# A delta-rule attention and ternary FFN kernel: the ternary product moved ahead of F's turn, and half of the values' product into the place it leaves

## The chip, the cores and the metric

The kernel runs on one core of one Trainium2 chip. The metric is the device time of one launch, in microseconds (us). The engines are TensorE (PE; its weight loads are shown as PEld), VectorE (DVE), ScalarE (ACT), GpSimd (POOL) and SyncE (SP), which here issues the DMAs. All arithmetic is in 32-bit floats.

## The reference

The input x is 4 sequences of 4096 tokens of 512 channels. Two blocks follow each other, each with a layernorm before it, a layernorm of its output, and a residual sum.

```python
def attn(x):                      # 16 heads of 32 channels
    rk = heads(x) / norm(heads(x));  wk = rk one token later
    v = heads(x @ Wv.T);  gate = sigmoid(x @ Wg.T);  beta = sigmoid(x @ Wb.T)
    # over the tokens, per sequence and head, S is 32 x 32:
    err = (v_t - wk_t @ S) * beta_t;  S = S + outer(wk_t, err);  o_t = (rk_t @ S) * gate_t
    return o @ Wo.T
def ffn(x):
    xn = layernorm(x) * ln_gamma + ln_beta
    w_q = clip(round(weight / mean(abs(weight))), -1, 1)        # ternary
    return clip(xn * 128 / max(abs(xn)), ...) @ w_q * scale
x = x + layernorm(attn(layernorm(x)))
x = x + layernorm(ffn(layernorm(x)))
```

## The kernel before

The token loop is cut into 128 units of 32 tokens. A unit holds all 4 sequences, so that its tokens fill the 128 partitions (4 x 32), and its 512 channels are the free dimension. Within a unit the recurrence is solved as a block: a triangular 32 x 32 matrix per sequence and head is inverted, and then only the state S (`state`) goes from unit to unit.

Two streams of units run side by side. The "unit of the blocks" (`AHEAD`, number k) does what doesn't need the state: the layernorm and the keys (`keys`, `keys_turn`: product `ps_hT`), the values and gates (`values`: `ps_v` at L251, 288 columns with both gates; `values_rest`: `ps_v` at L279, 256 columns; `values_out` multiplies each half by the key norms on DVE, L267), the Gram matrices of the keys (`grams`, L319), their copy out of PSUM on ACT (`blocks`, L330), and their masking on POOL (`writes` makes the mask `mb`, L290 to L294, from the gate tile `gb` of ACT, L256; `masked` applies it, L338). The "chain's unit" (`BACK`, number i, some 20 units behind) does what needs the state: `predict` (product `ps_r`, L439, and the difference `r` on DVE, L445), `apply` (the inverse times r: `ps_u`, L455, copied out as `ft` by ACT), `errors` (F's turn: the transposition `ps_f`, L468, from which DVE makes `e`, L471, and `o`, L476), `outputs` (o times the gate, POOL, L480), and `grow` (product `ps_ds`, L491, and four additions to the state on DVE, L497). Units behind the chain's unit are carried on through the output product (`project`, `ps_wo`, L534), the first residual (`residual`, DVE, L543, which needs `rstd_b` of POOL), the second norm, the ternary product (`ternary_a` and `ternary_b`, two of the four `ps_y` matmuls each, L593) and the second residual (`finish`, DVE, L612, with `rstd_y` of POOL).

The inverses of several units (8 in the steady stretch) are made together on DVE, as 30 pairs of a product `pr` (L364) and a sum `na` (L370), and one copy of a diagonal (L375). They are spread over 8 steps: `inverses(share)` in the plan issues the next instructions until the share of the step is used up. An instruction isn't cut, so a share runs over by up to one instruction, and the next one begins later for it.

The order is written out by hand. For each step the tuple `plan` is walked, and each function's instructions are chained behind those before it on the same engine, so each engine runs its own instructions in the plan's order and waits by semaphores for the other engines. The first steps that have a chain's unit are double: each is followed by the tuple `beside`, which does one more unit of the blocks. From some 20 units before the end the tuple `late` is used, which has no unit of the blocks.

PSUM is held as four single banks (tag `bank`) and one group of four banks (tag `quad`, for `ps_gram` and `ps_ds` in turn). A product waits until the last reader of the bank it is given has finished.

Of the kernel before, what the change touches and what calls it, by code (L numbers as in the profile page):

```python
# [22 lines left out]
def kernel(  # L23
# [91 lines left out]
    with ExitStack() as ph1:  # L115
# [35 lines left out]
        half = D // 2  # L151
# [535 lines left out]
        def ternary_centre():  # L687
# [13 lines left out]
        BACK, AHEAD = "chain's unit", "unit of the blocks"  # L701
# [3 lines left out]
            (BACK, -3, x1_turn),  # L705
            (BACK, 0, apply), (BACK, -3, x1_scale), (AHEAD, -1, masked),
            (AHEAD, 1, key_sums), (AHEAD, 3, x_stats), (AHEAD, 1, key_norms),
            (AHEAD, 2, keys), (AHEAD, 2, key_squares), 0.38,
            (BACK, -4, ternary_a), (BACK, 0, errors), (BACK, -4, ternary_b), (BACK, 0, outputs),
            (AHEAD, 3, x_norm), 0.2, (BACK, 0, grow), (BACK, -2, x1_stats),  # L710
            (AHEAD, 2, keys_turn), (AHEAD, -1, gates_first), (AHEAD, -2, gates), (BACK, 1, rekey), (BACK, -4, finish),
            (BACK, -1, project), (BACK, -3, largest), 0.36, (BACK, -2, x1_norm),
            (BACK, -1, residual), (AHEAD, 0, values), (AHEAD, 0, values_out, half),
            (AHEAD, 0, writes), (AHEAD, 0, values_rest), 0.06, (AHEAD, 0, values_out, 0),
            (AHEAD, 0, grams),
        )

        late = (
# [282 lines left out]
```

## Time and profile before

| | us |
|---|---|
| median of 3 runs | 2315.33 (2312.81 to 2315.37) |
| the profiled execution | 2311.62 |
| its span, first to last instruction | 2309.9 |
| PE busy | 2219.5 (96%) |
| DVE busy | 2027.3 (88%) |
| ACT busy | 1554.6 (67%) |
| POOL busy | 1528.3 (66%) |
| 16 DMA engines, mean share in q1 | 71.7% |

The mean granted clock of TensorE is 0.986. A busy time is a sum over stages with different limits. The page's slices show a start of some 130 us before the chain's first unit, a stretch of double steps up to about 320 us, single steps with a few stalls up to about 510 us, a steady stretch up to about 1976 us, and the late steps and the end.

### The profile page before, as it was taken

What the parts mean: (1) busy time and instruction counts of PE and PEld (TensorE: products, weight loads), DVE (VectorE), ACT (ScalarE), POOL (GpSimd) and SP (SyncE); (2) the same over time, 40 slices, a digit from 0 to 9 for tenths busy, and PEclk for the clock granted to TensorE, in tenths of its full rate; (3) what the DMA queues carried; (4) which work ended last, traced back from release to release, by engine and by line L of the source; (5) the groups of instructions that cost most, each with busy time, mean ns of one, the idle gap of its engine ahead of it and who ended that gap; (6) DMA issues with size and microseconds to landing.
All of it is one profiled execution on the core that took longest, in us unless ns stands there. A gap on an engine that the chain in (4) does not pass through costs nothing.

```text
span 2309.9 us, 60163 instructions
## 1 busy us (share of the span) xinstructions
PE 2219.5 (96%) x22563; PEld 1450.3 (63%) x22563; DVE 2027.3 (88%) x3069; ACT 1554.6 (67%) x3613; POOL 1528.3 (66%) x2057
## 2 busy tenths in 40 slices
PE   6688999999999999999999999999999999999997
PEld 5565666666666666666666666666666666655553
DVE  6898988999898998989989898899899898899853
ACT  6556676776776767767767677676776767655554
POOL 5787886777776776767767677676776766532221
PEclk9889999999999999999999999999999999999999
DMA  5586686777868777787877778677886967666652
GB/s 171 134 215 190 190 215 205 190 196 206 198 198 205 206 193 211 194 201 216 188 210 201 201 197 204 212 189 208 203 207 196 207 206 191 182 174 179 179 162 81
DMA packets 757202, 445.29 MB, mean 193 GB/s; under 512 B 582928, under 2 KB 582928, under 8 KB 756912
## 3 DMA queue, kind: packets, MB, share of 16 engines
q1 hardware_dynamic: 756528, 440.92, 71.7%
q8 instruction: 179, 2.93, 0.6%
q14 instruction: 111, 0.91, 0.1%
q10 hardware_dynamic: 384, 0.52, 0.1%
HBM read 205.07 MB, written 235.14 MB: 191 GB/s over the span
## 4 chain that ended last, share of the span: by engine, by line
PE 82%; DVE 11%; POOL 2%; issue 2%; DMA 2%; ACT 1%; SPq 1%; ACTq 0%; DVEq 0%; POOLq 0%
PE ps_wo L534 18%; PE ps_y L593 16%; PE ps_v L251 10%; PE ps_v L279 8%; PE ps_ds L491 6%; PE ps_gram L319 5%; PE ps_r L439 5%; PE ps_u L455 4%; DVE pr L364 3%; PE ps_hT L196 3%; PE ps_oT L514 2%; DVE na L370 2%; PE ps_f L468 2%; PE ps_xn L514 2%; DVE st_a L110 1%
## 5 line engine op out<-in xcount | busy, mean ns | idle before, releaser
L593 PE MATMUL ps_y<-wq,xn 128*128 128x512 f32 x1024 | 494.6, 606 | 0.0
L330 ACT COPY nat<-ps_gram 32x512 f32<-32x512 f32 x512 | 295.3, 577 | 286.6 <-PE ps_gram L319 276.1
L364 DVE TENSOR_TENSOR pr<-na 128x336 f32<-128x336 f32 (+25 forms) x540 | 461.2, 854 | 11.3
L370 DVE TENSOR_TENSOR na<-na,pr 128x336 f32<-128x336 f32 (+25 forms) x540 | 459.2, 850 | 12.2
L534 PE MATMUL ps_wo<-woT,oT 128*128 128x512 f32 x1024 | 464.0, 596 | 0.7 <-ACT oT L527 0.7
L231 POOL TENSOR_TENSOR rn<-ss,mhalf 128x16 f32<-128x16 f32 x128 | 440.7, 3443 | 10.7
L497 DVE TENSOR_TENSOR state<-ps_ds,state 32x512 f32<-32x512 f32 x508 | 348.4, 686 | 19.7 <-PE ps_ds L491 13.5
L338 POOL TENSOR_TENSOR nat<-nat,mb 128x512 f32<-128x512 f32 x122 | 159.5, 1307 | 290.6 <-issue 223.7
L534 PEld LDWEIGHTS ps_wo<-woT,oT 128*128 128x128 f32 x1024 | 185.3, 191 | 188.2 <-issue 184.7
L251 PE MATMUL ps_v<-wvbT,hN 128*128 128x288 f32 x1024 | 279.2, 417 | 14.3 <-POOL hN L207 14.2
L593 PEld LDWEIGHTS ps_y<-wq,xn 128*128 128x128 f32 x1024 | 174.5, 190 | 149.3 <-issue 146.0
L251 PEld LDWEIGHTS ps_v<-wvbT,hN 128*128 128x128 f32 x1024 | 198.1, 195 | 110.8 <-issue 28.2
L279 PE MATMUL ps_v<-wvbT,hN 128*128 128x256 f32 x1024 | 243.4, 381 | 0.0
L99 POOL TENSOR_TENSOR rstd_b<-vpe_b,mhalf 128x1 f32<-128x1 f32 x128 | 104.9, 820 | 186.3 <-ACT vpe_b L105 186.3
L279 PEld LDWEIGHTS ps_v<-wvbT,hN 128*128 128x128 f32 x1024 | 195.8, 191 | 34.3 <-DVE xr L543 0.4
L445 DVE TENSOR_TENSOR r<-v,ps_r 128x512 f32<-128x512 f32 x128 | 87.8, 686 | 135.0 <-PE ps_r L439 134.9
L520 ACT ACTIVATE junk_b<-ps_wo 128x512 f32<-128x512 f32 x128 | 76.5, 598 | 191.9 <-PE ps_wo L534 191.9
L491 PEld LDWEIGHTS ps_ds<-e,h 32*128 32x128 f32 x4064 | 127.3, 189 | 115.3 <-DVE e L471 91.1
L575 ACT ACTIVATE xn<-ps_xn,lnb,lng 128x128 f32<-128x128 f32 x512 | 193.6, 466 | 0.0
L491 PE MATMUL ps_ds<-e,h 32*128 32x128 f32 x4064 | 151.8, 286 | 19.3 <-DVE e L471 19.2
L319 PEld LDWEIGHTS ps_gram<-hT 32*128 32x128 f32 x4096 | 126.6, 187 | 39.5 <-issue 16.0
L319 PE MATMUL ps_gram<-hT 32*128 32x128 f32 x4096 | 151.1, 284 | 0.0
(153 smaller groups left out, 3867.6 us busy)
## 6 DMA issues: line engine op xcount, KB each, us to landing
x<-in_L_attn_x_dram SPq DMA_DIRECT2D x256, 128.0 KB
hT_d<-hT SPq DMA_DIRECT2D x128, 256.0 KB
v_d<-v SPq DMA_DIRECT2D x128, 256.0 KB
nat_d<-nat SPq DMA_DIRECT2D x128, 256.0 KB
na<-nat_d SPq DMA_DIRECT2D x256, 128.0 KB
q_d<-na SPq DMA_DIRECT2D x64, 512.0 KB
v<-v_d SPq DMA_DIRECT2D x128, 256.0 KB
hT<-hT_d SPq DMA_DIRECT2D x128, 256.0 KB
```

Of the source, the lines that this page charges most:

```text
L231: nc.gpsimd.tensor_tensor(rn, ss, mhalf, ALU.pow)
L251: nc.tensor.matmul(ps[:, : half + 2 * H], lhsT=my["hN"][:, k, :], rhs=wvbT[:, k, half:], start=(k == 0), stop=(k == KC - 1),)
L279: nc.tensor.matmul(ps[:, :half], lhsT=my["hN"][:, k, :], rhs=wvbT[:, k, :half], start=(k == 0), stop=(k == KC - 1),)
L319: nc.tensor.matmul(ps[:, j, q * P : (q + 1) * P], lhsT=hT[rows, q, :], rhs=hT[rows, q, :], start=True, stop=True,)
L330: nc.scalar.copy(nat[s].rearrange("p (j q) t -> p j q t", j=HQ), ps[s].rearrange("p j (q t) -> p j q t", q=NQ)[:, :, :, s],)
L364: nc.vector.tensor_tensor(prs[s], bcast(na[:, :, s, s + 1 :], [P, np_, s, m], 2), bcast(na[:, :, :s, s], [P, np_, s, m], 3), ALU.mult,)
L370: nc.vector.tensor_tensor(na[:, :, :s, s + 1 :], na[:, :, :s, s + 1 :], prs.pop(s), ALU.add)
L491: nc.tensor.matmul(psd[:, b, q * P : (q + 1) * P], lhsT=h[s, q * P : (q + 1) * P], rhs=e[s, q * P : (q + 1) * P], start=True, stop=True,)
L497: nc.vector.tensor_tensor(S[s, :, :, s], psd[s].rearrange("p b (q d) -> p b q d", q=NQ)[:, :, :, s], S[s, :, :, s], ALU.add,)
L534: nc.tensor.matmul(ps, lhsT=oT[:, k, :], rhs=woT[:, k, :], start=(k == 0), stop=(k == KC - 1))
L575: nc.scalar.activation(xn[:, k * P : (k + 1) * P], ps[:, k * P : (k + 1) * P], AF.Identity, bias=lnb[:, k : k + 1], scale=lng[:, k : k + 1],)
L593: nc.tensor.matmul(my["ps_y"], lhsT=my["xn"][:, k * P : (k + 1) * P], rhs=wq[:, k, :], start=(k == 0), stop=(k == KC - 1),)
```

## The change

Only the tuple `plan` is changed; the functions and the tuples `lead`, `beside` and `late` are as they were. The ternary product's four matmuls are issued together ahead of F's turn. `values`, which is the first half of the values' product with the gates, is issued behind F's turn. Its DVE part `values_out(half)` follows, ahead of the state's growth. `values_rest` is issued ahead of `residual`. The inverses' shares of a step go from 0.38, 0.2, 0.36, 0.06 to 0.48, 0.12, 0.34, 0.06.

```diff
-            (AHEAD, 2, keys), (AHEAD, 2, key_squares), 0.38,
-            (BACK, -4, ternary_a), (BACK, 0, errors), (BACK, -4, ternary_b), (BACK, 0, outputs),
-            (AHEAD, 3, x_norm), 0.2, (BACK, 0, grow), (BACK, -2, x1_stats),
-            (AHEAD, 2, keys_turn), (AHEAD, -1, gates_first), (AHEAD, -2, gates), (BACK, 1, rekey), (BACK, -4, finish),
-            (BACK, -1, project), (BACK, -3, largest), 0.36, (BACK, -2, x1_norm),
-            (BACK, -1, residual), (AHEAD, 0, values), (AHEAD, 0, values_out, half),
-            (AHEAD, 0, writes), (AHEAD, 0, values_rest), 0.06, (AHEAD, 0, values_out, 0),
-            (AHEAD, 0, grams),
+            (AHEAD, 2, keys), (AHEAD, 2, key_squares), 0.48,
+            (BACK, -4, ternary_a), (BACK, -4, ternary_b), (BACK, 0, errors), (AHEAD, 0, values),
+            (BACK, 0, outputs), (AHEAD, 3, x_norm), 0.12, (AHEAD, 0, values_out, half),
+            (BACK, 0, grow), (BACK, -2, x1_stats), (AHEAD, 2, keys_turn),
+            (AHEAD, -1, gates_first), (AHEAD, -2, gates), (BACK, 1, rekey), (BACK, -4, finish),
+            (BACK, -1, project), (BACK, -3, largest), 0.34, (BACK, -2, x1_norm),
+            (AHEAD, 0, values_rest), (BACK, -1, residual), (AHEAD, 0, writes), 0.06,
+            (AHEAD, 0, values_out, 0), (AHEAD, 0, grams),
```

## The prediction

> **What bounds the kernel now.** First the page: which engine is full.
>
> ```profile
> PE 2219.5 (96%) x22563; PEld 1450.3 (63%) x22563; DVE 2027.3 (88%) x3069; ACT 1554.6 (67%) x3613; POOL 1528.3 (66%) x2057
> ```
>
> TensorE is, with DVE next. Then busy time by stretches, to see where TensorE still idles (stretch, length, PE, PEld, DVE, ACT, POOL, clock, DMA share, GB/s).
>
> ```profile
> 130.00:320.00 190.00, 170.27 (x1776) 122.47 (x1776) 172.32 (x284) 125.15 (x277) 157.26 (x200) 0.95 0.76 198
> ...
> 510.50:1976.00 1465.50, 1463.44 (x15123) 958.21 (x15127) 1325.80 (x1937) 1033.57 (x2408) 1039.98 (x1376) 1.00 0.76 202
> ```
>
> In the 86 steady steps TensorE idles 2 us of 1465, so no order of the same products can gain there. From one `r` to the next a step takes 17.01 us, in one step of eight 17.25. The double steps (130 to 320) have 20 us of idle. Third, who waits for whom.
>
> ```profile
> DVE r L445 <- PE ps_r L439: 134.9, 113, 1.7
> ...
> PEld ps_ds L491 <- DVE e L471: 91.1, 95, 4.8
> ...
> PE ps_ds L491 <- DVE e L471: 19.2, 23, 4.6
> ```
>
> DVE waits for `ps_r` ahead of `r`, in 113 of 128 steps, 1.2 us each. This is DVE's whole reserve. If DVE is later than that, `ps_u`, which needs `r`, stops TensorE. Last, the timeline of DVE in the steady step with the least reserve, and of POOL at its end.
>
> ```profile
> 1090.06 0.69 DVE L445 TENSOR_TENSOR r<-v,ps_r 128x512 f32<-128x512 f32 x1 [1.38 <-PE ps_r L439]
> ...
> 1094.90 0.68 DVE L471 TENSOR_TENSOR e<-ps_f,bet 128x512 f32<-128x512 f32 x1
> ...
> 1097.27 2.79 DVE L497 TENSOR_TENSOR state<-ps_ds,state 32x512 f32<-32x512 f32 x4
> 1100.09 0.75 DVE L612 SCALAR_TENSOR_TENSOR xr<-ps_y,rstd_y,xr 128x512 f32<-128x512 f32 x1
> ...
> 1101.35 1.15 DVE L364 TENSOR_TENSOR pr<-na 128x960 f32<-128x960 f32 x1
> 1102.54 1.16 DVE L370 TENSOR_TENSOR na<-na,pr 128x960 f32<-128x960 f32 x1
> 1103.61 0.74 DVE L543 SCALAR_TENSOR_TENSOR xr<-ps_wo,rstd_b,xr 128x512 f32<-128x512 f32 x1
> 1104.27 0.41 DVE L267 TENSOR_TENSOR v<-ps_v,nrm 128x256 f32<-128x256 f32 x1
> 1104.61 1.64 DVE L364 TENSOR_TENSOR pr<-na 128x960 f32<-128x960 f32 x1
> 1106.17 0.41 DVE L267 TENSOR_TENSOR v<-ps_v,nrm 128x256 f32<-128x256 f32 x1
> 1107.08 0.69 DVE L445 TENSOR_TENSOR r<-v,ps_r 128x512 f32<-128x512 f32 x1 [0.50 <-PE ps_r L439]
> ```
>
> ```profile
> 1102.36 0.55 POOL L99 TENSOR_TENSOR rstd_b<-vpe_b,mhalf 128x1 f32<-128x1 f32 x1 [0.92 <-ACT vpe_b L105]
> 1103.48 0.30 POOL L290 TENSOR_TENSOR bet<-gb,rn 128x16 f32<-128x16 f32 x1 [0.57 <-ACT gb L256]
> ...
> 1104.15 1.08 POOL L294 TENSOR_TENSOR mb<-bet,mneg 128x512 f32<-128x512 f32 x1
> ...
> 1111.03 3.78 POOL L231 TENSOR_TENSOR rn<-ss,mhalf 128x16 f32<-128x16 f32 x1
> ```
>
> DVE is busy without a break from `r` to the wait of 0.50. The product at 1104.61 took 1.64 us where its like took 1.15: POOL's mask product ran from 1104.15 to 1105.23, and the inverse's product ended 1.02 after it.
>
> **The change, part by part, steady step.** Times count from the end of `r`; TensorE's slots are the start-to-start distances of the trace.
>
> *TensorE.* `ps_u` starts at 0.2, the ternary product at 1.2. Before: two matmuls 1.82, F's turn 0.44, two matmuls 1.81, so `ps_ds` at 5.3. After: four matmuls 3.53, F's turn at 4.7 for 0.44, half of the values (eight passes of 0.24, and 0.1) 2.0, so `ps_ds` at 7.2. Then `ps_ds` 1.10, `ps_hT` 0.50, `ps_wo` 3.44, other half 1.82, `ps_gram` 1.11, `ps_r` 1.01, `ps_oT` 0.49, `ps_xn` 0.53: 17.02 as before. Nothing is removed; nothing is gained but waits.
>
> *The wait for `e`.* DVE's 0.48 is about 0.7 us more of the inverse ahead of `e`. Summing each of the eight steps' instructions, DVE is ready for `e` at 4.2 to 5.35, F's turn ends at 5.3. So `e` starts near 5.37 and ends at 6.05, 1.2 us before `ps_ds`. The stall of 0.24 in one step of eight goes: 11 times 0.24, and two of 0.12, is -2.9.
>
> *The state's growth.* Its additions began 6.5 after `r`; now they can't begin before `ps_ds` has been made, 7.2 + 1.25 = 8.46 (1.25 is start of `ps_ds` to first addition where the addition waits). This is 1.94 later in the least-reserve step. `o` ends at 6.65, at most two pieces of the inverse and the 0.41 of the moved values' half fit before 8.46 (latest end 8.2), so these are free, but DVE idles up to 0.7 there.
>
> *From the growth to `r`.* DVE must be ready at 16.33, when `ps_r` is done. The growth to the end of the inverse's third share is unchanged in the step shown: additions 8.46, `finish` 11.28, maximum 11.94, product 12.54, sum 13.72 to 14.88, residual 14.79. Now the values' half is gone behind it (-0.33 by starts), so the piece of the last share starts at 15.46. POOL: `rstd_b` follows `ps_wo`, which ends 1.94 later, so it starts at 13.55 and ends at 14.1. `bet` no longer waits for `gb`, which is ready by 7.5. It is issued at once, but meets the sum of 13.72 to 14.88. In the trace such a small product of POOL ends 0.08 after DVE's instruction, and the mask follows 0.47 after that instruction (13.62 to 14.09 in the step from 1073.7): here at 15.35, 0.11 ahead of the piece at 15.46. So the mask goes first, until 16.43, and the piece ends 1.02 later, at 17.45; the last values' half 0.33 more: `r` at 17.7, 1.36 late. `ps_oT` and `ps_xn` cover 0.13. Stall 1.23 us, once in eight steps.
>
> In the step with the diagonal's copy, the copy of 0.41 meets the mask likewise: `r` at 16.6, stall 0.16. In the step with 0.98, 0.98 and 1.03 in the third share, 16.51: stall 0.05. The other five are ready at 15.5 to 16.0: none. Sum 1.44 x 11 = +15.8, with the -2.9: **+13**.
>
> *Steps from 320 to 510.* Here DVE is already last in three (17.9 to 19.2 us) and next to it in others. Where a piece stands behind the residual it meets the mask as above (0.5 to 1 each in five or six steps), and in others the later growth adds 0.6. I sum +6; bounds 0 and +9.
>
> *Double steps.* There `ps_ds` waits up to 2.9 us for `e`, and the values' half, moved into that wait, no longer stands between it and the next `ps_r`. At most 1.94 comes out of each. But DVE, or POOL at `rstd_y` and `rstd_b`, is next: by the step from 271.7, DVE is ready at 22.65 where `r` came at 23.43. Over eight such steps 0.3 to 1.1 each, **-5**; bounds 0 and -10.
>
> *Queues.* On SP the small gate DMA (0.67) goes ahead of `hT_d` and no longer waits late; the residual's and the values' stores are issued up to 1.9 later, the fetches behind them too. SP idles some 3.7 us of each step ahead of the residual's store, and these fetches are for two steps on: 0. On ACT the ternary squares leave the growth's region, the gate's sigmoid (0.20) comes in with a wait until 7.3: `hT`'s copy ends at 9.5 instead of 8.2, read steps later: 0. If the fetch's cover failed, each late fetch would show in `ps_u`; I allow +20 in a rival. The late steps and the end are unchanged: 0.
>
> *A rule against it.* The inverse's extra piece ahead of `e` runs beside POOL's power `rn`, 3.78 us from 1111.03. The trace has a sum `na` of 1.14 us at 1113.13 inside it, not lengthened. The Trainium skill, "SBUF — State Buffer", section "SBUF: two separate sides", says that DVE with two SBUF inputs and a GpSimd instruction exclude each other for the whole instruction. By it the extra piece would wait until 7.0, `e` end at 8.8 and `ps_ds` be 1.6 late, in about five steps of eight: some +90. By the row, 0. I take the row for the power, and the measured 1.64 for the mask.
>
> **Sum.** +13 + 6 - 5 = +14. The span becomes 2324, the execution 2311.6 + 14 = 2325.6. That profile ran 3.7 below the median of the runs, so on the median 2315.3 + 14 = **2329 us**.
>
> **The rivals.** About 0.2% (4.6 us) is what a measurement here can tell from no change.
> - *As summed*, 2329: 0.50.
> - *The piece goes ahead of the mask.* The margin is 0.11 us. Then the piece runs 15.46 to 16.6, `r` is late 0.55, stall 0.42: 0.63 x 11 - 2.9 = +4; +3 up to 510, -5 before: +2 to +5, 2319. For it: small margin. Against: POOL's distance of 0.47 repeats to 0.01. 0.17, half of it within 0.2%.
> - *Faster: DVE's reserve is enough.* Place: the wait ahead of `r`. It decides when the growth begins at 7.1 or earlier, or the mask is over before the residual (then nothing is late). Then steady -2.9, early -5 to -7: 2307. For it: the mean reserve of 1.2. Against: 0.50 in the step shown. 0.13.
> - *The waits only change places*, 2315: 0.05.
> - *A new wait as well*: the residual held by POOL's `rstd_b` where that is stretched (1.26 us in some steps), or fetches late on SP. +35, 2350: 0.15.
>
> The order of instructions does change as described, so that the change does nothing is no rival of its own. Faster 0.13, within 0.2% 0.13, slower 0.74. The range leaves out most of the last rival and the best of the faster ones: 2310 to 2345.
>
> **What would show it.** Right: growth near 8.4 after `r`; no wait of `ps_ds` for `e` in the steady stretch; the wait ahead of `r` down from 135 us to some 40; PE waiting for `r` at `ps_u`, above all one step in eight of some 18.2 us; the lone product behind the residual at 2.0 us or more. Wrong: all steps at 17.01, or a stall at another place than `ps_u`.

## The result, and the profile after

The changed kernel takes 2323.59 us (median of 6 runs, 2322.65 to 2325.47) against 2314.46 us (6 runs, 2312.40 to 2315.37). The ratio is 1.0048, with an interval of 1.0037 to 1.0058. It is slower by 9.1 us; 14 had been forecast, and the forecast's range held it. The profiled spans are 2321.7 and 2309.9 us, 11.8 apart: the profiled execution of the kernel before was a short one, 2.8 below the median of its runs. Differences by stretches below are of single profiles.

The first line of the page after: busy times differ little but for DVE's, which is 21 us more at the same number of instructions. Some of its instructions have become longer.

```profile
PE 2217.8 (96%) x22563; PEld 1446.2 (62%) x22563; DVE 2048.2 (88%) x3069; ACT 1562.7 (67%) x3613; POOL 1529.9 (66%) x2057
```

Busy time by stretches, first after, then before. The three stretches are the double steps, the single steps up to the steady stretch, and the 85 steady steps, each cut at a start of `r`, so that a line of after holds the work of the line of before.

```profile
128.50:316.40 187.90, 167.94 (x1772) 118.75 (x1772) 171.22 (x284) 124.00 (x276) 158.92 (x202) 0.97 0.77 200
316.40:527.50 211.10, 205.06 (x2111) 133.65 (x2112) 192.60 (x292) 144.55 (x336) 149.26 (x202) 1.00 0.72 194
527.50:1987.00 1459.50, 1447.05 (x14960) 947.52 (x14959) 1330.73 (x1917) 1030.00 (x2380) 1029.58 (x1361) 1.00 0.76 201
```

```profile
129.80:319.30 189.50, 169.74 (x1772) 122.05 (x1772) 171.82 (x283) 124.52 (x277) 156.84 (x199) 0.95 0.76 198
319.30:527.60 208.30, 204.43 (x2110) 133.53 (x2111) 191.77 (x292) 143.38 (x335) 152.79 (x202) 1.00 0.73 197
527.60:1976.70 1449.10, 1447.04 (x14962) 947.48 (x14962) 1310.32 (x1916) 1022.14 (x2381) 1028.05 (x1360) 1.00 0.76 202
```

The steady stretch lost 10.4 us, at a TensorE busy time that is equal to 0.01 us: all of the loss is time in which TensorE idles. The double steps gained 1.6, the steps between lost 2.8, the start before the first `r` gained 1.3 (it lies between 128.0 and 129.8 us in all profiles of this study, so this is hardly the change). The five steps in which the blocks' units run out lost 1.4 (78.0 to 79.4 us by the starts of `r`), and the 17 after them are equal.

Who waited for whom, after:

```profile
DVE state L497 <- PE ps_ds L491: 46.0, 92, 1.6
PEld ps_u L455 <- DVE r L445: 43.3, 120, 1.9
...
DVE r L445 <- PE ps_r L439: 27.9, 59, 0.7
...
PE ps_u L455 <- DVE r L445: 21.4, 21, 1.6
...
PEld ps_ds L491 <- DVE e L471: 12.2, 11, 3.7
```

DVE's reserve ahead of `r` went from 134.9 to 27.9 us. TensorE's wait for `e` fell (on the side of the weight loads 91.1 to 12.2, and no steady step has it), and in its place TensorE waits for `r` at `ps_u`, 21.4 us in 21 steps, 11 of them the long steps of the steady stretch. DVE's longer wait is ahead of the growth, 46.0 us for 13.5. The timeline of DVE, of POOL and of TensorE in the step that answers to the one of the prediction, which now takes 18.37 us:

```profile
1102.81 2.79 DVE L497 TENSOR_TENSOR state<-ps_ds,state 32x512 f32<-32x512 f32 x4 [0.48 <-PE ps_ds L491]
...
1108.07 1.16 DVE L370 TENSOR_TENSOR na<-na,pr 128x960 f32<-128x960 f32 x1
1109.15 0.75 DVE L543 SCALAR_TENSOR_TENSOR xr<-ps_wo,rstd_b,xr 128x512 f32<-128x512 f32 x1
1109.81 1.97 DVE L364 TENSOR_TENSOR pr<-na 128x960 f32<-128x960 f32 x1
1111.70 0.41 DVE L267 TENSOR_TENSOR v<-ps_v,nrm 128x256 f32<-128x256 f32 x1
1112.04 0.67 DVE L445 TENSOR_TENSOR r<-v,ps_r 128x512 f32<-128x512 f32 x1
```

```profile
1107.89 0.55 POOL L99 TENSOR_TENSOR rstd_b<-vpe_b,mhalf 128x1 f32<-128x1 f32 x1 [2.79 <-ACT vpe_b L105]
1108.41 0.90 POOL L290 TENSOR_TENSOR bet<-gb,rn 128x16 f32<-128x16 f32 x1
...
1109.69 1.07 POOL L294 TENSOR_TENSOR mb<-bet,mneg 128x512 f32<-128x512 f32 x1
```

```profile
1112.76 1.08 PE L455 MATMUL ps_u<-tbd,r 128*32 128x128 f32 x32 [1.13 <-DVE r L445]
```

`bet` waited until the sum `na` had ended at 1109.23 (0.90 for 0.22), the mask began at 1109.69, 0.12 ahead of DVE's product at 1109.81, and the product took 1.97 us where its like takes 1.15. `r` came 0.82 later for it, and that with the later growth made TensorE stand 1.13 us.

### The profile page after: what moved, and what is told of

Its sections match the earlier page's. It is cut to its first block, busy times and chain, and to the rows that moved or that the text cites. A ratio compares the mean times of both kernels' runs of the same rounds, so it can differ in the third digit from the quotient of the medians.

```text
span 2321.7 us, 60420 instructions
## 1 busy us (share of the span) xinstructions
PE 2217.8 (96%) x22563; PEld 1446.2 (62%) x22563; DVE 2048.2 (88%) x3069; ACT 1562.7 (67%) x3613; POOL 1529.9 (66%) x2057
## 4 chain that ended last, share of the span: by engine, by line
PE 76%; DVE 13%; POOL 4%; issue 3%; ACT 2%; DMA 2%; SPq 1%; ACTq 0%; DVEq 0%; POOLq 0%
PE ps_y L593 18%; PE ps_wo L534 15%; PE ps_v L251 9%; PE ps_v L279 6%; PE ps_ds L491 6%; PE ps_u L455 5%; PE ps_r L439 4%; PE ps_gram L319 4%; DVE pr L364 4%; DVE state L497 3%; PE ps_oT L514 2%; PE ps_f L468 2%; PE ps_hT L196 2%; DVE na L370 2%; PE ps_xn L514 2%
## 5 line engine op out<-in xcount | busy, mean ns | idle before, releaser
L364 DVE TENSOR_TENSOR pr<-na 128x336 f32<-128x336 f32 (+25 forms) x540 | 484.2, 897 | 12.5
L593 PE MATMUL ps_y<-wq,xn 128*128 128x512 f32 x1024 | 477.8, 606 | 0.0
L370 DVE TENSOR_TENSOR na<-na,pr 128x336 f32<-128x336 f32 (+25 forms) x540 | 444.6, 823 | 11.8
L231 POOL TENSOR_TENSOR rn<-ss,mhalf 128x16 f32<-128x16 f32 x128 | 430.1, 3360 | 10.7
L99 POOL TENSOR_TENSOR rstd_b<-vpe_b,mhalf 128x1 f32<-128x1 f32 x128 | 87.8, 686 | 355.6 <-ACT vpe_b L105 355.5
L593 PEld LDWEIGHTS ps_y<-wq,xn 128*128 128x128 f32 x1024 | 183.0, 190 | 199.8 <-issue 196.6
L279 PEld LDWEIGHTS ps_v<-wvbT,hN 128*128 128x128 f32 x1024 | 195.1, 191 | 73.4 <-issue 48.3
L251 PEld LDWEIGHTS ps_v<-wvbT,hN 128*128 128x128 f32 x1024 | 189.8, 195 | 75.4 <-POOL hN L207 31.5
L455 PE MATMUL ps_u<-tbd,r 128*32 128x128 f32 x4096 | 139.7, 277 | 26.0 <-DVE r L445 21.4
L480 POOL TENSOR_TENSOR o<-o,gr 128x512 f32<-128x512 f32 x128 | 152.0, 1188 | 8.2 <-DVE o L476 8.1
## 6 DMA issues: line engine op xcount, KB each, us to landing
x<-in_L_attn_x_dram SPq DMA_DIRECT2D x256, 128.0 KB
na<-nat_d SPq DMA_DIRECT2D x256, 128.0 KB
```

The costliest lines, as they stand in the source:

```text
L231: nc.gpsimd.tensor_tensor(rn, ss, mhalf, ALU.pow)
L251: nc.tensor.matmul(ps[:, : half + 2 * H], lhsT=my["hN"][:, k, :], rhs=wvbT[:, k, half:], start=(k == 0), stop=(k == KC - 1),)
L279: nc.tensor.matmul(ps[:, :half], lhsT=my["hN"][:, k, :], rhs=wvbT[:, k, :half], start=(k == 0), stop=(k == KC - 1),)
L364: nc.vector.tensor_tensor(prs[s], bcast(na[:, :, s, s + 1 :], [P, np_, s, m], 2), bcast(na[:, :, :s, s], [P, np_, s, m], 3), ALU.mult,)
L370: nc.vector.tensor_tensor(na[:, :, :s, s + 1 :], na[:, :, :s, s + 1 :], prs.pop(s), ALU.add)
L455: nc.tensor.matmul(ps[quarters(j), qq * P : (qq + 1) * P], lhsT=r[:, hd * DH : (hd + 1) * DH], rhs=tbd[:, j * NQ + qq, :], start=True, sto ...
```

## The experiments

Each timed run has a kernel before beside it on the same chip; ratios are to that.

**E1. The mask early.** One line of the plan: `writes` ahead of the output product.

```diff
-            (BACK, -1, project), (BACK, -3, largest), 0.34, (BACK, -2, x1_norm),
-            (AHEAD, 0, values_rest), (BACK, -1, residual), (AHEAD, 0, writes), 0.06,
+            (AHEAD, 0, writes), (BACK, -1, project), (BACK, -3, largest), 0.34, (BACK, -2, x1_norm),
+            (AHEAD, 0, values_rest), (BACK, -1, residual), 0.06,
```

> The changed kernel, with POOL's mask product issued ahead of the output product instead of behind the residual. gb is ready by then, so POOL should make the mask near 11.3 to 12.4 us after r, where DVE makes finish and the maximum. Theory (the inverse's piece behind the residual waits for the mask): that piece takes 1.15 us instead of some 2.1, the long step of eight goes from 18.37 to some 17.4 us, and the time falls by about 9 us in the steady stretch and 1 to 3 in the steps before it, to 2312 to 2315. Rival (the state's growth 1.9 us later is all of it, the mask only fills a wait): the long step stays at 18.4 and the time within 2 us of the changed kernel's 2323.6.

Measured: 2319.85 us, ratio 1.003 (1.0018 to 1.0042), 3.7 us below the changed kernel. The time is above what was expected, and the double steps are why. The steady stretch did as expected: 1450.4 us, 9.1 less than the changed kernel's 1459.5, and the long step 17.55. The timelines of DVE and POOL there:

```profile
1111.08 0.74 DVE L543 SCALAR_TENSOR_TENSOR xr<-ps_wo,rstd_b,xr 128x512 f32<-128x512 f32 x1
1111.74 1.15 DVE L364 TENSOR_TENSOR pr<-na 128x960 f32<-128x960 f32 x1
```

```profile
1107.59 1.08 POOL L294 TENSOR_TENSOR mb<-bet,mneg 128x512 f32<-128x512 f32 x1
1109.83 0.55 POOL L99 TENSOR_TENSOR rstd_b<-vpe_b,mhalf 128x1 f32<-128x1 f32 x1 [1.15 <-ACT vpe_b L105]
```

With the mask over at 1108.67 the same product takes 1.15 us. But the double steps went from 187.9 to 194.2 us. There POOL has little idle time (it is 85% busy in this stretch of the changed kernel), and `rstd_b` now stands behind the mask, with the residual behind it. From a double step, DVE and POOL:

```profile
266.09 0.75 DVE L543 SCALAR_TENSOR_TENSOR xr<-ps_wo,rstd_b,xr 128x512 f32<-128x512 f32 x1 [2.06 <-POOL rstd_b L99]
```

```profile
264.49 1.07 POOL L294 TENSOR_TENSOR mb<-bet,mneg 128x512 f32<-128x512 f32 x1
265.52 0.54 POOL L99 TENSOR_TENSOR rstd_b<-vpe_b,mhalf 128x1 f32<-128x1 f32 x1
```

The same residual waited 0.43 us in the changed kernel.

**E8. The mask early in single steps only.** It takes E1's miss apart. An item of the plan that ends in `None` is passed over in double steps. In single steps the later `writes` then does nothing, since the plan issues each function once for a unit.

```diff
+                if item[-1] is None:
+                    if double:
+                        continue
+                    item = item[:-1]
...
-            (BACK, -1, project), (BACK, -3, largest), 0.34, (BACK, -2, x1_norm),
+            (AHEAD, 0, writes, None), (BACK, -1, project), (BACK, -3, largest), 0.34, (BACK, -2, x1_norm),
```

> The changed kernel with the mask issued early in single steps only; double steps as in the changed kernel. With the mask early in all steps the double steps took 194.2 instead of 187.9 us, since rstd_b, and with it the residual, stood behind the mask on POOL. Theory: the double steps are back at 188, the steady stretch stays at 1450: 2312 to 2315. Rival (the early mask costs POOL's other work in single steps too): 2316 to 2320.

Measured: 2312.40 us against 2312.40, ratio 1.0000 (0.9992 to 1.0009). The stretches took 189.0, 209.2 and 1450.5 us. So in single steps the place of POOL's three instructions for the mask (`bet` twice and `mb`) is worth all that the change had lost. The steady stretch, which has 7 us less DVE busy time than the changed kernel's:

```profile
526.90:1977.40 1450.50, 1447.08 (x14960) 947.48 (x14959) 1323.36 (x1917) 1030.01 (x2380) 1002.00 (x1360) 1.00 0.77 202
```

**E2. No piece behind the residual.** The last share goes to the third; the mask stays.

```diff
-            (BACK, -1, project), (BACK, -3, largest), 0.34, (BACK, -2, x1_norm),
-            (AHEAD, 0, values_rest), (BACK, -1, residual), (AHEAD, 0, writes), 0.06,
+            (BACK, -1, project), (BACK, -3, largest), 0.4, (BACK, -2, x1_norm),
+            (AHEAD, 0, values_rest), (BACK, -1, residual), (AHEAD, 0, writes), 0.0,
```

> The changed kernel with the shares 0.48, 0.12, 0.40, 0: no piece of the inverse stands behind the residual, the mask stays where it is. Theory: the same piece made ahead of the residual doesn't meet the mask; r is ready at some 17.0 where ps_r is done at 16.33, so the long step is some 17.5 us, and the time is 2313 to 2317. Rival (later growth alone): DVE's sum from the growth to r is the same to 0.1 us, so the long step stays near 18.4 and the time at 2322 to 2325.

Measured: 2314.03 us, ratio 1.0004 (0.9996 to 1.0013). The long step is 17.67 us, for 17.5 expected. But another step of eight, the one with the diagonal's copy, went from 17.01 to 17.54, so the steady stretch is 1455.6, 3.9 below the changed kernel's; the double steps, at 184.4, gave 3.5 more. DVE's product in the long step, ahead of the residual, then DVE's copy in that other step, and POOL's mask beside it:

```profile
1102.21 1.16 DVE L364 TENSOR_TENSOR pr<-na 128x960 f32<-128x960 f32 x1
1103.28 0.74 DVE L543 SCALAR_TENSOR_TENSOR xr<-ps_wo,rstd_b,xr 128x512 f32<-128x512 f32 x1
...
622.70 1.10 DVE L375 COPY na<-diag 128x128 f32<-128x128 f32 x1
```

```profile
622.53 1.13 POOL L294 TENSOR_TENSOR mb<-bet,mneg 128x512 f32<-128x512 f32 x1
```

So here the copy meets the mask: it took 1.10 us, for 0.28 in E8, where the mask is long over.

E1 and E2 leave the growth where the change put it, and both bring the long step to within 0.7 us of its floor. So of the 1.36 us above 17.01 about 0.8 is the mask (18.37 to 17.55). The rest goes with the later growth and the DVE work that is left behind it.

**E3. More of the inverse ahead of the growth.** Shares 0.54, 0.14, 0.32, 0.

```diff
-            (AHEAD, 2, keys), (AHEAD, 2, key_squares), 0.48,
+            (AHEAD, 2, keys), (AHEAD, 2, key_squares), 0.54,
...
-            (BACK, 0, outputs), (AHEAD, 3, x_norm), 0.12, (AHEAD, 0, values_out, half),
+            (BACK, 0, outputs), (AHEAD, 3, x_norm), 0.14, (AHEAD, 0, values_out, half),
...                                   # and 0.34 to 0.32, 0.06 to 0.0
```

> The changed kernel with the shares 0.54, 0.14, 0.32, 0: more of the inverse ahead of e and ahead of the growth, where DVE idles after the change, less behind it. Theory: summing each of the eight steps, r is ready at 15.1 to 15.9, always ahead of 16.33, and e starts by 5.6, ahead of the 6.4 at which ps_ds would wait; so all steady steps take 17.01 to 17.02, and the time is 2307 to 2312, below the kernel before. Rival (something other than DVE's work behind the growth holds r, such as late fetches on SP): long steps stay, 2320 or more.

Measured: 2305.88 us, ratio 0.9970 (0.9958 to 0.9982). That is 1.1 below the range expected; the steady steps are as expected. Busy time in its steady stretch:

```profile
523.60:1969.70 1446.10, 1446.10 (x14961) 947.68 (x14962) 1322.94 (x1915) 1031.81 (x2381) 1042.60 (x1361) 1.00 0.77 202
```

TensorE has no gap in 1446.1 us, 85 steps of 17.01. The growth is as late as in the changed kernel (8.46 us after `r` in most steps), so a late growth alone costs nothing here: it costs with the DVE work that stands between it and the next `r`.

**E4. The ternary product alone.** The kernel before, with its four ternary matmuls together ahead of F's turn.

```diff
-            (BACK, -4, ternary_a), (BACK, 0, errors), (BACK, -4, ternary_b), (BACK, 0, outputs),
+            (BACK, -4, ternary_a), (BACK, -4, ternary_b), (BACK, 0, errors), (BACK, 0, outputs),
```

> The kernel before with only the ternary product issued whole ahead of F's turn; values, shares and all else as before. Theory: ps_ds follows F's turn directly, e ends some 0.9 us after the slot in which ps_ds would start, so TensorE waits 0.9 us in nearly each of about 100 steps: 2390 to 2410. Rival (DVE is late for e in any case, and the wait is hidden): within 10 us of the kernel before.

Measured: 2398.38 us, ratio 1.0365 (1.0349 to 1.0381). A steady step takes 17.86 us, 0.85 more. From who waited for whom:

```profile
PE ps_ds L491 <- DVE e L471: 97.2, 111, 4.1
```

So the values' half is the cover of `e`, which the second ternary half was before.

**E5. The new order with the old shares.** 0.38, 0.2, 0.36, 0.06.

> The changed kernel's order with the old shares 0.38, 0.2, 0.36, 0.06: one part of the change alone. Theory: the single piece behind the residual still meets the mask, so the long step of 18.4 us stays, and the larger third share makes three more of the eight steps late by 0.1 to 0.2 us. Steady stretch some 14 us above the kernel before, time 2324 to 2330. Rival (the loss comes from the new shares): near the kernel before, 2311 to 2316.

Measured: 2343.85 us, ratio 1.0132 (1.0116 to 1.0147). The sign is as expected, the size is twice that: the steady stretch took 1471.8 us, 22.7 above the kernel before where 14 was expected, and the steps between 217.6 for 208.3. The long step is there (18.38), and the step with the diagonal's copy takes 18.02. In that step the growth begins 9.36 us after `r`, for 8.72 in the changed kernel, and the timelines of DVE and POOL say why:

```profile
1041.63 0.60 DVE L364 TENSOR_TENSOR pr<-na 128x432 f32<-128x432 f32 x1
1042.27 1.34 DVE L370 TENSOR_TENSOR na<-na,pr 128x432 f32<-128x432 f32 x1
```

```profile
1042.01 1.13 POOL L480 TENSOR_TENSOR o<-o,gr 128x512 f32<-128x512 f32 x1
```

Between `o` and the growth stands POOL's gate product; a second piece of the inverse there runs into it. The sum `na` took 1.34 us there, where one of this size takes about 0.6. What was expected had no such meeting in it. The share of 0.12 in the change keeps most of the inverse out of that place.

**E6. New shares in the old order.** The kernel before with 0.34, 0.24, 0.42, 0.

> The kernel before, its order untouched, with the shares 0.34, 0.24, 0.42, 0: less of the inverse ahead of e, no piece behind the residual. It shows what shares alone can give in the old order. Theory: DVE is ready for e by 4.3 us after r in all eight steps and ready for r by 15.4, both in time, so the stall of 0.25 us per eight steps goes: 2309 to 2313, some 2 to 3 us below the kernel before. Rival (the old order needs its early inverse pieces): at or above the kernel before.

Measured: 2311.03 us, ratio 0.9987 (0.9981 to 0.9994), as expected: steady stretch 1446.5, double steps 187.2, but the steps between them 211.4 for 208.3. The old order too can reach TensorE's floor in the steady stretch, so there the new order gives nothing that shares don't. E3 is lower than E6 in the steps between, 208.0 for 211.4.

**E7. The new order, shares by kind of step.** E3's in single steps, E2's in double ones.

> The new order with the shares 0.54, 0.14, 0.32, 0 in single steps and 0.48, 0.12, 0.40, 0 in double steps, by what the two earlier variants took in each stretch (double steps 187.0 against 184.4 us). Theory: the stretches add, so 2.6 us come off the variant with 0.54 throughout: 2302 to 2305. Rival (what a double step leaves undone is paid later): 2305 to 2308.

Measured: 2304.34 us (2302.44 to 2307.04), ratio 0.9964 (0.9952 to 0.9976), the lowest time of the study; its runs and E3's overlap, so between these two nothing is settled by time. Its profile has 184.4 us for the double steps and 1446.1 for the steady ones.

## Why the prediction was right

*The long step.* Forecast: a stall of 1.23 us in one step of eight. Measured: 18.37 in place of 17.01, with the next step at 16.85, 1.20 net. The chain was as written: growth at 8.46 (trace 8.46), `bet` behind the sum, mask at 15.35 (15.34), the product at 15.46 (15.46), `r` at 17.7 (17.69). E1 and E8, with the mask early, and E2, with the product early, show its cause by taking the meeting away in two ways. The order of mask and product hung on 0.11 us, and the prediction gave it no more than even odds.

*The other steps of eight.* The step with 0.98, 0.98 and 1.03 was 17.20 with 16.86 after it, 0.04 net for 0.05. The step of the diagonal's copy was forecast at 0.16 and took none: there `bet` fitted between DVE's short pieces, so the mask began at 14.73, about 0.5 sooner than a start of `r` at 16.6 implies. That and the stall of 0.25 that went give 1.0 per eight steps; the steady stretch measured +10.4, forecast 13.

*The steps up to 510.* Forecast +6, measured +2.8 by 527. The losses came as written: with E8's early mask five of these steps are 0.5 to 0.85 us shorter, 3.5 together (18.94 to 18.41, 18.52 to 17.67 and so on), so the meeting is there, and two others are some 0.5 longer than before in both, as forecast for the later growth. What the sum put at nothing is a gain: with the mask out of the way the three steps in which DVE was last are 0.3 to 0.75 shorter than before (17.67 for 18.32). In the kernel before, TensorE's matmuls waited for `e` in four of these steps, 2.4 us together, and after the change in none. That this is the gain is read from the traces; no run shows it alone.

*The double steps.* Forecast -5, measured -1.6, and even that is little more than scatter: E8, with the same order there, took 189.0 for 187.9. Who TensorE waited for up to 320 us, before and after:

```profile
PE ps_ds L491 <- DVE e L471: 13.8, 6, 4.6
```

```profile
PE ps_v L251 <- POOL hN L207: 5.0, 5, 2.3
PE ps_ds L491 <- DVE e L471: 4.3, 3, 3.2
PE ps_u L455 <- DVE r L445: 3.0, 2, 1.6
```

The wait for `e` fell by 9.5 us, as the forecast meant it to. Most of that came back at two places: at the moved product itself, which needs `hN` of POOL, and at `r`. The prediction named POOL as a limit here, but at `rstd_y` and `rstd_b` and not at `hN`, and took its size from DVE alone. In one double step (24.96 us for 23.80) the time even rose. There DVE's `finish` waited 1.88 us for `rstd_y`, 1.26 before, and the piece behind the residual met the mask (1.28 us, for 0.95 before). E2, with the same wait of 1.88 and its piece ahead of the residual, took 23.79. E2's and E7's 184.4 for the stretch are what was forecast, but with other shares.

*What was costed at nothing.* The late steps are equal. The five steps where the blocks' units end lost 1.4, which no term held; E1 has the same there, so it isn't the mask. No wait at `ps_u` is put down to a fetch. On the rule that the prediction set aside: the power `rn` ran from 1097.59 for 3.78 us, and the added sum ahead of `e` took 1.15 us at 1098.61 inside it. Taking the row and not the rule was worth some 90 us of forecast, by the prediction's own estimate.

*The total.* By spans the terms came to +10.4, +2.8 and -1.6, with -1.3 at the start and +1.4 near the end, about 11.8 in all for 14. Loss and gain were both forecast too large, by 5.8 and 3.4, so that the total lies nearer than its terms is in part luck. The cause and the place of the steady loss are not.

*The rivals.* That DVE's reserve would be enough is out, by 21 waits at `ps_u`; that the piece would be ahead of the mask is out by 0.12 us in the trace. E1 is close to that rival made real: its long step with the next is 0.39 above two usual ones, for 0.42, and its steady stretch is 1.3 above before, for +4. That waits only change places is out by the interval of the ratio. The new wait at the residual didn't come: it waited for `rstd_b` 12.8 us in 9 steps, before 11.0 in 9.

## What to carry to other kernels

When TensorE is full, a reordering that only moves its products can win nothing but waits, and what it does to the engine behind must be summed step by step: here the growth came 1.9 us later, against a mean reserve of 1.2 us a step. Where instructions of two engines hold each other back, ask which of them now meet: one meeting in eight steps, 0.8 us each time, was nearly the whole loss of the steady stretch. Other shares of the filler work turned a loss of 9 us into a gain of 7 (E3). Test such a move in each stretch of the program apart: the early mask gained 9 us in one and lost 6 in another.

## What the runs showed of the hardware

POOL's instructions didn't all keep DVE out. These are counts from the changed kernel's trace from 320 us on, of the inverse's products and sums on DVE, which read two SBUF operands. Of 16 that began during POOL's mask product (128 x 512, 1.07 us) 15 became longer, as the 1.97 for 1.15 above; of 24 that began during the gate product all did. The diagonal's copy was held back too (1.10 for 0.28, E2). But of 228 that began during the long power (128 x 16), none took over 0.03 us more than the shortest of its size.

In the other direction POOL waited for DVE (counts of the whole trace). A 128 x 16 product of POOL that began during such an instruction of DVE ended 0.08 to 0.09 us after it in 194 of 213 cases; the other 19 were not lengthened. The power, begun during one, ended 2.78 to 2.81 us after it, and begun with none it mostly took 2.93. So its 3.8 us in the steps shown hold a wait of about 1 us at its start.
